# Table rows fetched by index instead of by one-hot products, and the last step of every layer norm on another engine

## The chip, the cores and the metric

The kernel runs on one core of one Trainium2 chip. A core has five engines that each work through a list of instructions of their own: TensorE (PE in the profile: matrix products, and transposes done as products with the identity), VectorE (DVE), ScalarE (ACT: activation functions and copies), GpSimd (POOL) and SyncE (SP, which here only starts transfers). Sixteen DMA engines move data. PE writes to a small accumulator memory (PSUM); everything else is in on-chip SBUF or in the chip's main memory (HBM). The metric is the time of one execution on the device in microseconds (us): the median of three runs.

## The reference, cut to what matters

One decoder layer over `x` of 4 batches x 1024 tokens x 256 features, in float32: grouped-query attention (16 heads, 4 key/value heads), cross attention to 64 context tokens, and a feed-forward stage that picks one of 64 "tiles" per token. A layer norm without scale stands before each stage, and one more with scale closes the feed-forward stage:

```python
x = x + attn(layernorm(x))            # 16 heads of 64, softmax over 1024 keys
x = x + cross_attn(layernorm(x), ctx) # 16 heads of 16, 64 keys
x = x + ffn(layernorm(x))

def ffn(xf):                          # per token
    cluster = argmax(calibrate(xf @ cluster_sigs.T))        # of 8
    local   = argmax(calibrate(xf @ sigs.T)[cluster])       # of 8
    tile    = cluster * 8 + local
    comp = tanh(gelu(xf @ w1c + b1c) @ w2c + b2c)           # 2 numbers
    hh   = relu(comp @ spline_w1[tile] + spline_b1[tile])   # 16 numbers
    mag  = hh @ spline_w2[tile] + spline_b2[tile]
    y    = xf + mag * directions[tile] * output_scale
    return layernorm(y) * gamma + beta
```

All parameters of one tile are laid in one row of `table`: 2x16 + 16 + 16 + 1 + 256 = 321 numbers, 64 rows.

## The kernel before

Tokens are worked on in tiles of 128. For each batch, layer norm 1 (`normed`, groups of two tiles) gives the transposed input `xT`; `queries`, `keys` and `value_rows` project it. `duo(b, d)` is the unit of attention: four heads of one token tile. PE makes the scores (L577), DVE the row maxima (L591), ACT the exponentials (L597); the weights are then transposed, in three duos of four by DVE in 32x32 blocks (L606) with sixteen SP transfers that carry the blocks to their place (L633), in the fourth by PE (L616) with ACT copies (L620); PE multiplies them with the values (L656). `project` (L709 to L716) closes a token tile. Every two token tiles `cross_attention` follows (layer norm 2), every four `feed_forward` (layer norms 3 and 4; two tiles at a time for the last four of the last batch). So there are nine calls of `feed_forward`, seven of four tiles and two of two.

The parts that the change touches:

- `layernorm` (L390 to L416) is three tasks. `stats` on DVE gives mean and variance of each tile (L401, L402). `rsqrt` on POOL adds eps (L406) and raises to the power -1/2 (L407). `apply` on DVE computes (x - mean) * rs, one instruction of 128x256 a tile (L412). It is called 16 times with two tiles for layer norm 1, 16 times with two for layer norm 2, 32 times with one for layer norm 3 and 32 times with one for layer norm 4: 96 calls, 128 tiles.
- `feed_forward` (L991 to L1155): after the routing, `hot` holds for each token a one-hot row of 64 (L1075). PE transposes it (`flip_hot`, L1089), ACT copies it out (L1092), and per token tile PE multiplies it with `tab`, the table in SBUF (L1097), which picks the row of 321 numbers; ACT copies that to `par` (L1100). DVE then evaluates the spline (L1116 to L1127), adds the result to the stage's input (L1131), and layer norm 4 follows. `finish` on POOL (L1146 to L1148) scales, shifts and adds the residual, and a POOL transfer stores the result (L1153).
- `tab` is loaded once, by SP, at L281, after the other weights and before the first residual tile and the third group of layer norm 1's input.

The order on every engine is fixed by a planner before the program runs. `Flow.add` takes for each task an engine, a planned cost in us, a key and the buffers it reads and writes; `Flow.order` (L120) then simulates the engines: it always emits the task that can start earliest, and among equals urgent tasks first, then the lowest key. `lag` is the planned time from a task's end to the moment that its result can be used by another engine. Each engine later works through its list in that order and waits where a planned time turns out too short. `places` is the number of buffers of each kind: three PSUM banks `p1` are shared by most small products, one `par`, one `hot`.

Of the kernel before, what the change touches and what calls it, by code (L numbers as in the profile page):

```python
# [10 lines left out]
F32 = mybir.dt.float32  # L11
U8 = mybir.dt.uint8
AF = mybir.ActivationFunctionType
ALU = mybir.AluOpType
# [3 lines left out]
P = 128  # L18
# [10 lines left out]
NTILES, NCL, TPC, GRID, COMP, NK = 64, 8, 8, 16, 64, 8  # L29
NS = NCL + NTILES  # L30
GW = 4 * GRID + 1
GT = GW + D
# [160 lines left out]
def decoder(  # L193
# [21 lines left out]
    nc = tc.nc  # L215
    const = ctx.enter_context(tc.tile_pool(name="const", bufs=1))
    big = ctx.enter_context(tc.tile_pool(name="big", bufs=1))
    work = ctx.enter_context(tc.tile_pool(name="work", bufs=2))
    small = ctx.enter_context(tc.tile_pool(name="small", bufs=4))
# [4 lines left out]
    mm, flip = nc.tensor.matmul, nc.tensor.transpose  # L224
# [1 line left out]
        dict(  # L226
            s=2, p1=3, o=1, x=3, xn1=2, xT=1, kT0=1, kT1=1, vn=4, qT=12, prob=2, probT=2, sums=3, nmax=4,
            heads=1, rb=1, rsum=2, res=1, ln=2, xxT=1, xqT=1, kblk=1, vblk=1, xkt=1, xvt=1, xsc=1,
            xmx=2, xpT=1, xrs=2, xo=1, xoT=1, xf=1, fxT=1, hT=1, sc=1, comp=2, cal=1, fm=4, hot=1, hotT=1,
            par=1, hh=1, mag=2,  # L230
        ),
        {"p1", "ln", "res", "rb", "rsum", "nmax"},
    )
    add = flow.add

# [4 lines left out]
    def psum1(name):  # L240

        return Buf("p1", lambda: ps_1.tile([P, 512], F32, tag="p1", name=name))
# [4 lines left out]
    def load(name, shape, src, engine, key, lag, dtype=F32, via=None):  # L247
        t = const.tile(shape, dtype, name=name)
        b = Buf()
        q = nc.sync if engine == "SP" else nc.scalar  # L250
        for k, (dst, s) in enumerate(via(t, src) if via else [(t, src)]):
            add(engine, 0.5, key, lambda dst=dst, s=s: q.dma_start(out=dst, in_=s), writes=[b], lag=lag)
        return t, b
# [24 lines left out]
    sraw, sraw_ = weight("sraw", sig_rawT, DC, NTILES, "SP", -33, 8)  # L278
    cw1, cw1_ = weight("cw1", c_w1, DC, COMP, "SP", -32, 8)
    cw2, cw2_ = load("cw2", [COMP, 2], c_w2, "SP", -31, 8)  # L280
    tab, tab_ = load("tab", [NTILES, GT], table, "SP", -30, 8)  # L281

    def row(name):
        a, b = ROW_AT[name]
# [105 lines left out]
    def layernorm(key, name, src, dst, w, reads, writes):  # L390

        st = Buf("ln", lambda: (
            small.tile([P, w, 6], F32, tag="bnst", name=f"{name}_st", bufs=2),
            small.tile([P, w, 2], F32, tag="bnmv", name=f"{name}_mv", bufs=2),
            small.tile([P, w], F32, tag="bnrs", name=f"{name}_rs", bufs=2),
        ))

        def stats():
            bn, mv, _ = st.t
            for t in range(w):  # L400
                nc.vector.bn_stats(bn[:, t, :], src(t))  # L401
                nc.vector.bn_aggr(mv[:, t, :], bn[:, t, :])  # L402

        def rsqrt():
            _, mv, rs = st.t
            nc.gpsimd.tensor_scalar(rs, mv[:, :, 1], EPS, None, ALU.add)  # L406
            nc.gpsimd.tensor_tensor(rs, rs, minus_half.to_broadcast([P, w]), ALU.pow)  # L407

        def apply():
            _, mv, rs = st.t  # L410
            for t in range(w):
                nc.vector.tensor_scalar(dst(t), src(t), mv[:, t, 0:1], rs[:, t : t + 1], ALU.subtract, ALU.mult)  # L412

        add("DVE", 0.6 * w, key, stats, reads, [st], holds=writes)
        add("POOL", 1.0, key, rsqrt, [st], [st])
        add("DVE", 0.41 * w, key, apply, [st, *reads], writes)  # L416

    def transposed(key, name, src, dst, k, reads, write):

# [131 lines left out]
    def duo(b, d):  # L551
# [3 lines left out]
        if e == 0:  # L555
            sums[b, qt] = buf("sums", small, H, name=f"sums_{b}_{qt}")
            heads[b, qt] = buf("heads", work, QC, P, name=f"heads_{b}_{qt}")
        ss = sums[b, qt]
        prob = Buf("prob", lambda: work.tile([P, 4 * S], F32, tag="prob", name=f"prob_{b}_{d}"))
        probT = Buf("probT", lambda: work.tile([P, 4 * S], F32, tag="probT", name=f"probT_{b}_{d}"))  # L560

# [84 lines left out]
        for part in range(2):  # L646
            def values(part=part):
                for kc in range(4 * part, 4 * part + 4):
                    for z, r in enumerate(halves):
                        j = 2 * jp + z  # L650
                        if by_array(d):
                            rhs = probT.t.rearrange("p (z c x) -> p z c x", z=2, c=NT)[:, z, kc]
                        else:
                            rhs = probT.t.rearrange("p (b z i c q) -> p b z i c q", b=4, z=2, i=2, q=32)[:, :, z, :, kc]
                            rhs = rhs.rearrange("p b i q -> p i b q")
                        mm(  # L656
                            av.t[r, :],
                            lhsT=vns[b, kc // 2].t[:, kc % 2, j * HD : (j + 1) * HD],
                            rhs=rhs,
                            start=(kc == 0),  # L660
                            stop=(kc == NT - 1),
                        )

            add(
                "PE", 1.9, at + 1, values,
                [probT.part((z, part)) for z in range(2)] + [vns[b, 2 * part], vns[b, 2 * part + 1]] + [av] * part,
                [av],
                holds=[heads[b, qt]],
            )

        rs = buf("rsum", small, 4, name=f"rsum_{b}_{d}")
# [319 lines left out]
    def feed_forward(b, t0, w, at):  # L991
# [50 lines left out]
        def route():  # L1042
# [18 lines left out]
        hot = Buf("hot", lambda: (  # L1061
            small.tile(wide, F32, tag="hot", name=f"hot_{name}", bufs=1),
            small.tile([P, w, TPC], F32, tag="sel", name=f"sel_{name}", bufs=2),
        ))

        def c_wide():
            return ch.t[1].unsqueeze(3).to_broadcast(wide)

        def select():
            h, sel = hot.t  # L1070
            nc.vector.tensor_tensor(h, sc.t[:, :, NCL:].rearrange("p t (c j) -> p t c j", j=TPC), c_wide(), ALU.mult)
            nc.vector.tensor_reduce(sel, h.rearrange("p t c j -> p t j c"), AX.X, ALU.add)

        def chosen():
            nc.vector.tensor_tensor(hot.t[0], lh.t[1].unsqueeze(2).to_broadcast(wide), c_wide(), ALU.mult)  # L1075

        add("DVE", 1.0, at + 6, select, [sc, ch], [hot])
        c, gates = calibrated(at + 7, f"cl_{name}", lambda: hot.t[1], w, [hot])
# [1 line left out]
        add("DVE", 0.45, at + 9, chosen, [lh, ch, hot], [hot])  # L1080


        hotT = Buf("hotT", lambda: big.tile([NTILES, n], F32, tag="hotT", name=f"hotT_{name}"))
        par = Buf("par", lambda: big.tile([P, w, GT], F32, tag="par", name=f"par_{name}"))
        pt = psum1(f"pht_{name}")

        def flip_hot():
            for k in range(w):
                flip(pt.t[:NTILES, k * P : (k + 1) * P], hot.t[0][:, k].rearrange("p c j -> p (c j)"), ident)  # L1089

        add("PE", 0.14 * w, at + 10, flip_hot, [hot], [pt], holds=[hotT])
        add("ACT", 0.6, at + 10, lambda: nc.scalar.copy(hotT.t, pt.t[:NTILES, :n]), [pt], [hotT])  # L1092
        for t in range(w):
            pg = psum1(f"pg_{name}_{t}")

            def gather(t=t, pg=pg):
                mm(pg.t[:, :GT], lhsT=hotT.t[:, t * P : (t + 1) * P], rhs=tab, start=True, stop=True)  # L1097

            def evict(t=t, pg=pg):
                nc.scalar.copy(par.t[:, t, :], pg.t[:, :GT])  # L1100

            add("PE", 0.6, at + 11, gather, [hotT, tab_], [pg], holds=[par])
            add("ACT", 0.45, at + 11, evict, [pg], [par.part(t)])


        hh = Buf("hh", lambda: (
# [169 lines left out]
```

## Time and profile before

The median of three runs is 1993.22 us (1990.15 to 1993.29). The profiled execution took 1997.92 us, 1996.2 us of it from its first to its last instruction (the span).

| | busy us | share of the span | instructions |
|---|---|---|---|
| PE, matrix products | 1864.4 | 93% | 11204 |
| DVE | 1538.9 | 77% | 2447 |
| ACT | 964.2 | 48% | 1730 |
| POOL | 267.2 | 13% | 422 |

How to read the lines that follow: a group of instructions is named by line, engine, operation and tile, `out<-in`, with partitions x elements of each, the number of instructions, then the busy time and the mean of one in ns, and then the time that the engine had stood idle just before them and what ended it. The chain of work that ended last is followed back from the last instruction, at each step to what released it. In a timeline the first two numbers are start and duration in us, and square brackets hold the idle time before. PEclk is the granted clock of PE, where 1.00 is full speed.

### The profile page before, as it was taken

How to read it: one execution, taken by the hardware profiler on the slowest of the kernel's cores; microseconds unless marked ns; L12 is line 12 of the kernel's file. 1: busy time of each engine (PE TensorE's matmuls, PEld its weight loads, DVE VectorE, ACT ScalarE, POOL GpSimd, SP SyncE). 2: the span in 40 equal slices, each digit the busy share in tenths (PEclk: the TensorE clock that was granted, in tenths of full speed). 3: DMA queues.
4: the chain of work that ended last, by engine and by line, in shares of the span. 5: the costliest groups of instructions: out<-in, count | busy, mean ns of one | idle time of the engine just before them, and what ended most of it. 6: DMA issues, size and time to landing. Idle time of an engine off the chain costs nothing.

```text
span 1996.2 us, 30371 instructions
## 1 busy us (share of the span) xinstructions
PE 1864.4 (93%) x11204; PEld 1114.0 (56%) x11204; DVE 1538.9 (77%) x2447; ACT 964.2 (48%) x1730; POOL 267.2 (13%) x422
## 2 busy tenths in 40 slices
PE   7899999999999999989999999989999999997973
PEld 4455555655566555556556555655556655564542
DVE  4767787897788878787778878887778877778853
ACT  2545455555445555545445545454545554553431
POOL 1000101030010301121000311103001030010322
PEclk9899999999999999989999999998999999998975
DMA  3555554454455455545454456535455435545510
GB/s 132 127 127 137 127 132 109 105 121 108 104 127 117 94 122 123 123 110 127 96 116 107 95 128 137 122 75 127 96 122 127 101 91 127 113 100 127 119 24 5
DMA packets 87859, 220.92 MB, mean 111 GB/s; under 512 B 26336, under 2 KB 36896, under 8 KB 87712
## 3 DMA queue, kind: packets, MB, share of 16 engines
q1 hardware_dynamic: 85440, 212.42, 47.3%
q0 software_dynamic: 1168, 4.19, 0.6%
q8 instruction: 89, 1.46, 0.3%
q10 hardware_dynamic: 1104, 2.37, 0.3%
q14 instruction: 58, 0.48, 0.1%
HBM read 13.37 MB, written 4.19 MB: 9 GB/s over the span
## 4 chain that ended last, share of the span: by engine, by line
PE 81%; DVE 12%; ACT 3%; DMA 1%; issue 1%; SPq 1%; POOL 1%; POOLq 0%; ACTq 0%; DVEq 0%
PE s L577 25%; PE av L656 22%; DVE nmax L591 6%; PE pq L530 5%; PE po L709 5%; PE ptp L616 5%; PE rb L682 2%; PE xav L870 2%; PE xs L819 2%; PE pxq L797 2%; ACT prob L597 2%; PE pv L502 2%; DVE prob L606 1%; PE pk L479 1%; PE pg L1097 1%; PE pxp L900 1%
## 5 line engine op out<-in xcount | busy, mean ns | idle before, releaser
L597 ACT ACTIVATE prob<-s,nmax 128x1024 f32<-128x1024 f32 x512 | 569.2, 1115 | 581.0 <-DVE nmax L591 571.3
L591 DVE TENSOR_REDUCE nmax<-s 128x1 f32<-128x1024 f32 x512 | 602.1, 1217 | 211.4 <-PE s L577 210.6
L577 PE MATMUL s<-kT,qT 64*128 64x512 f32 x2048 | 545.4, 621 | 9.3 <-ACT prob L597 9.0
L656 PE MATMUL av<-probT,vn 128*64 128x256 f32 x4096 | 479.6, 385 | 2.7 <-DMA probT<-prob 2.5
L606 DVE STREAM_TRANSPOSE prob<-prob 128x1024 f32<-128x1024 f32 x384 | 460.3, 1225 | 20.5 <-ACT prob L597 15.3
L656 PEld LDWEIGHTS av<-probT,vn 128*64 128x64 f32 x4096 | 284.0, 137 | 204.1 <-issue 70.5
L577 PEld LDWEIGHTS s<-kT,qT 64*128 64x128 f32 x2048 | 196.2, 187 | 216.6 <-issue 170.2
L620 ACT COPY probT<-ptp 128x512 f32<-128x512 f32 x256 | 138.9, 594 | 127.7 <-PE ptp L616 127.7
L616 PE MATMUL ptp<-ident,prob 128*128 128x128 f32 x1024 | 147.6, 281 | 20.5 <-ACT probT L620 5.0
L616 PEld LDWEIGHTS ptp<-ident,prob 128*128 128x128 f32 x1024 | 109.9, 141 | 76.4 <-issue 31.2
L530 PE MATMUL pq<-ln_T,wq 128*128 128x256 f32 x512 | 132.2, 407 | 4.2 <-DMA wq<-in_w_qT 3.7
L837 POOL TENSOR_TENSOR xsc<-xsc,xmx 128x1024 f32<-128x1024 f32 x32 | 61.0, 1908 | 497.0 <-DVE xmx L834 252.6
L709 PE MATMUL po<-wo,heads 128*128 128x256 f32 x512 | 121.1, 386 | 1.9 <-DVE xsc L822 1.8
L530 PEld LDWEIGHTS pq<-ln_T,wq 128*128 128x128 f32 x512 | 99.2, 202 | 32.8 <-issue 15.0
L709 PEld LDWEIGHTS po<-wo,heads 128*128 128x128 f32 x512 | 94.2, 190 | 34.5 <-issue 15.9
L715 POOL TENSOR_TENSOR x<-x,res 128x256 f32<-128x256 f32 x32 | 23.3, 728 | 620.9 <-DVE res L712 516.6
L597 ACT ACTIVATION_READ_ACCUMULATOR prob<-s,nmax 128x1 f32 x512 | 100.8, 197 | 0.0
L541 ACT ACTIVATE qT<-pq,bqs,qscale 128x256 f32<-128x256 f32 x128 | 65.3, 563 | 49.6 <-PE pq L530 49.2
L695 DVE TENSOR_TENSOR heads<-av,rb 128x256 f32<-128x256 f32 x128 | 53.0, 414 | 46.7 <-PE av L656 45.6
L682 PEld LDWEIGHTS rb<-ident,rsum 128*64 128x64 f32 x1024 | 54.6, 136 | 59.0 <-issue 45.4
L682 PE MATMUL rb<-ident,rsum 128*64 128x128 f32 x1024 | 83.3, 284 | 4.2 <-DVE xres L903 4.2
L819 PE MATMUL xs<-kblk,xq 128*128 128x512 f32 x128 | 67.9, 653 | 1.7 <-ACT xq L806 1.7
(162 smaller groups left out, 1526.9 us busy)
## 6 DMA issues: line engine op xcount, KB each, us to landing
probT<-prob SPq DMA_DIRECT2D x1536, 128.0 KB, 2.3
ln_n<-in_x SPq DMA_DIRECT2D x16, 256.0 KB, 3.1
x<-in_x SPq DMA_DIRECT2D x8, 512.0 KB, 4.2
out<-ln_n POOLq DMA_DIRECT2D x7, 512.0 KB, 3.5
wo<-in_w_oT SPq DMA_DIRECT2D x1, 1024.0 KB, 13.3
wq<-in_w_qT ACTq DMA_DIRECT2D x1, 1024.0 KB, 9.6
rowv<-in_rows ACTq DMA_DIRECT2D x1, 774.0 KB, 11.7
xwkv<-in_xw_kv SPq DMA_DIRECT2D x1, 512.0 KB, 13.1
```

The lines of the kernel that those rows point to most:

```text
L530: mm(pq.t[:, 2 * P * k : 2 * P * (k + 1)], lhsT=wq[:, dc, (c + k) * P : (c + k + 1) * P], rhs=xTs[b].t[:, dc, 2 * P * w : 2 * P * (w + 1)] ...
L541: nc.scalar.activation(qTs[b, w, c + k].t, pq.t[:, 2 * P * k : 2 * P * (k + 1)], AF.Identity, bias=bqs[:, c + k : c + k + 1], scale=qscale,)
L577: mm(ps[z].t[:, 512 * g : 512 * (g + 1)], lhsT=q.t[r, (qt % 2) * P : (qt % 2 + 1) * P], rhs=kT.t[r, 512 * g : 512 * (g + 1)], start=True, ...
L591: nc.vector.tensor_reduce(nmax.t, ps[z].t, AX.X, ALU.max, negate=True)
L597: nc.scalar.activation(weights(prob.t, z, i), src, AF.Exp, bias=nmax.t, accum_out=ss.t[:, k : k + 1])
L606: nc.vector.transpose(t, t)
L616: flip(pt.t[:, j * P : (j + 1) * P], weights(prob.t, z, i)[:, kc * P : (kc + 1) * P], ident)
L620: nc.scalar.copy(to[:, z, 4 * g : 4 * g + 4, i, :], pt.t.rearrange("p (c q) -> p c q", q=P))
L656: mm(av.t[r, :], lhsT=vns[b, kc // 2].t[:, kc % 2, j * HD : (j + 1) * HD], rhs=rhs, start=(kc == 0), stop=(kc == NT - 1),)
L682: mm(pr.t[r, i * P : (i + 1) * P], lhsT=rs.t[:, k : k + 1].to_broadcast([P, HD]), rhs=ident, start=True, stop=True,)
L709: mm(po.t[:, :D], lhsT=hT.t[:, c, :], rhs=wo[:, c, :], start=(c == 0), stop=(c == QC - 1))
L819: mm(ps.t, lhsT=qT.t[:, c, k * P : (k + 1) * P], rhs=kblk.t[:, c], start=True, stop=True)
```

## The change

Two parts, and what goes with them.

- The one-hot row is not made any more. `chosen` computes the number of the tile instead, 72 - 8*a - b with a and b the two "falling" values of the maxima, and writes it as an integer. The transposes, the 64x321 products and both ACT copies go; per token tile POOL starts an indirect DMA that fetches, for each of the 128 tokens, the row of `table` in HBM that the integer names, straight into `par`. The planner is told 1.2 us of POOL for one and 3.0 us until it has landed. `tab` and its load go.
- `apply` of every layer norm becomes an ACT activation, Identity(rs * x + bias) with per-partition scale and bias. The bias, -mean * rs, takes two more POOL instructions in `rsqrt`; its planned cost stays at 1.0 us. The planned 0.41 us a tile on DVE become 0.45 on ACT.

The name `hd` and the changed order of a set of names alter nothing that is emitted.

```diff
-            ... hot=1, hotT=1,
+            ... hot=1,
             par=1, hh=1, mag=2,
         ),
-        {"p1", "ln", "res", "rb", "rsum", "nmax"},
+        {"p1", "ln", "res", "rsum", "nmax", "rb"},
...
-    tab, tab_ = load("tab", [NTILES, GT], table, "SP", -30, 8)
...
         def rsqrt():
             _, mv, rs = st.t
             nc.gpsimd.tensor_scalar(rs, mv[:, :, 1], EPS, None, ALU.add)
             nc.gpsimd.tensor_tensor(rs, rs, minus_half.to_broadcast([P, w]), ALU.pow)
+            nc.gpsimd.tensor_tensor(mv[:, :, 1], mv[:, :, 0], rs, ALU.mult)
+            nc.gpsimd.tensor_scalar(mv[:, :, 1], mv[:, :, 1], -1.0, None, ALU.mult)
 
         def apply():
             _, mv, rs = st.t
             for t in range(w):
-                nc.vector.tensor_scalar(dst(t), src(t), mv[:, t, 0:1], rs[:, t : t + 1], ALU.subtract, ALU.mult)
+                nc.scalar.activation(dst(t), src(t), AF.Identity, bias=mv[:, t, 1:2], scale=rs[:, t : t + 1])
...
-        add("DVE", 0.41 * w, key, apply, [st, *reads], writes)
+        add("ACT", 0.45 * w, key, apply, [st, *reads], writes)
...
             small.tile([P, w, TPC], F32, tag="sel", name=f"sel_{name}", bufs=2),
+            small.tile([P, w], F32, tag="tno", name=f"tno_{name}", bufs=1),
+            small.tile([P, w], mybir.dt.int32, tag="tile", name=f"tile_{name}", bufs=1),
...
         def chosen():
-            nc.vector.tensor_tensor(hot.t[0], lh.t[1].unsqueeze(2).to_broadcast(wide), c_wide(), ALU.mult)
+            _, _, no, idx = hot.t
+
+            nc.vector.scalar_tensor_tensor(no, ch.t[0], float(-TPC), lh.t[0], ALU.mult, ALU.subtract)
+            nc.vector.tensor_scalar(idx, no, float(NCL * TPC + NCL), None, ALU.add)
...
-        hotT = Buf("hotT", lambda: big.tile([NTILES, n], F32, tag="hotT", name=f"hotT_{name}"))
         par = Buf("par", lambda: big.tile([P, w, GT], F32, tag="par", name=f"par_{name}"))
-        pt = psum1(f"pht_{name}")
-
-        def flip_hot():
-            for k in range(w):
-                flip(pt.t[:NTILES, k * P : (k + 1) * P], hot.t[0][:, k].rearrange("p c j -> p (c j)"), ident)
-
-        add("PE", 0.14 * w, at + 10, flip_hot, [hot], [pt], holds=[hotT])
-        add("ACT", 0.6, at + 10, lambda: nc.scalar.copy(hotT.t, pt.t[:NTILES, :n]), [pt], [hotT])
         for t in range(w):
-            pg = psum1(f"pg_{name}_{t}")
-
-            def gather(t=t, pg=pg):
-                mm(pg.t[:, :GT], lhsT=hotT.t[:, t * P : (t + 1) * P], rhs=tab, start=True, stop=True)
-
-            def evict(t=t, pg=pg):
-                nc.scalar.copy(par.t[:, t, :], pg.t[:, :GT])
-
-            add("PE", 0.6, at + 11, gather, [hotT, tab_], [pg], holds=[par])
-            add("ACT", 0.45, at + 11, evict, [pg], [par.part(t)])
+            def gather(t=t):
+                nc.gpsimd.indirect_dma_start(
+                    out=par.t[:, t, :],
+                    out_offset=None,
+                    in_=table,
+                    in_offset=bass.IndirectOffsetOnAxis(ap=hot.t[3][:, t : t + 1], axis=0),
+                )
+
+            add("POOL", 1.2, at + 11, gather, [hot], [par.part(t)], lag=3.0)
```

## The prediction

> **What bounds the kernel now.** I read the page's busy times first, then the chain that ended last, then the busy times by stretch.
>
> ```profile
> PE 1864.4 (93%) x11204; PEld 1114.0 (56%) x11204; DVE 1538.9 (77%) x2447; ACT 964.2 (48%) x1730; POOL 267.2 (13%) x422
> ```
>
> ```profile
> PE 81%; DVE 12%; ACT 3%; DMA 1%; issue 1%; SPq 1%; POOL 1%; POOLq 0%; ACTq 0%; DVEq 0%
> ```
>
> ```profile
> 60.00:1900.00 1840.00, 1769.14 (x10797) 1052.70 (x10796) 1464.50 (x2218) 921.74 (x1654) 239.84 (x355) 0.98 0.51 115
> 1900.00:1996.20 96.20, 51.33 (x242) 33.04 (x240) 41.41 (x146) 22.93 (x42) 21.66 (x33) 0.67 0.02 8
> ```
>
> The columns of the last view are PE, weight loads, DVE, ACT and POOL busy, then granted clock and DMA share. From 60 to 1900 us PE is busy for 1769 of 1840 us, so PE time taken away there is worth nearly its full length, unless PE then waits for something else. The last 96 us are different: no engine is full, the clock is 0.67, and each step waits for the one before it. There, latency counts.
>
> The groups that the change removes or moves, the nearest rows for what it adds, and PE's longest wait:
>
> ```profile
> L1097 PE MATMUL pg<-tab,hotT 64*128 64x321 f32 x64 | 30.3, 604 | 4.3 <-ACT hotT L1092 2.2 <-DVE rb L691 1.2 <-ACT par L1100 0.8
> L1089 PE MATMUL pht<-ident,hot 128*64 128x128 f32 x32 | 6.3, 322 | 30.1 <-DVE hot L1075 30.1
> L1100 ACT COPY par<-pg 128x321 f32<-128x321 f32 x32 | 13.2, 432 | 22.1 <-PE pg L1097 21.8
> L412 DVE TENSOR_SCALAR ln_n<-x,ln_mv,ln_rs 128x256 f32<-128x256 f32 x64 | 24.2, 400 | 10.7 <-POOL ln_rs L407 10.7
> L541 ACT ACTIVATE qT<-pq,bqs,qscale 128x256 f32<-128x256 f32 x128 | 65.3, 563 | 49.6 <-PE pq L530 49.2
> L406 POOL TENSOR_SCALAR ln_rs<-ln_mv 128x1 f32<-128x1 f32 x64 | 14.0, 218 | 116.7 <-DVE ln_mv L402 109.9 <-DVE rsum L676 6.8
> L1153 POOL DMA_DIRECT2D out<-ln_n x9 | 7.6, 848 | 2.4 <-POOL ln_n L1148 2.4
> ```
>
> ```profile
> PE pht L1089 <- DVE hot L1075: 15.5, 3, 9.6
> ```
>
> That wait, 60 to 1900 us, is three waits for the one-hot row in three of the seven four-tile calls of feed-forward. PE's timeline shows one:
>
> ```profile
> 869.83 0.66 PE L1089 MATMUL pht<-ident,hot 128*64 128x128 f32 x4 [2.93 <-DVE hot L1075]
> 871.16 4.64 PE L1097 MATMUL pg<-tab,hotT 64*128 64x321 f32 x8 [0.67 <-ACT hotT L1092]
> 875.74 1.11 PE L426 MATMUL ln_pt<-ident,ln_n 128*128 128x128 f32 x4
> ```
>
> The eight products take 4.64 us here, 3.16 in the first call (390 to 420 us): between 872 and 880 us the clock is 0.50.
>
> **What the Trainium skill says.** (1) "ScalarE: Activation LUTs", section "What ACT_TABLE_LOAD costs": 186 ns + 0.833 ns an element, about 93 ns more for each per-partition operand, and 93 ns of overlap back to back. For 256 elements with scale and bias that is an estimate of 585 ns; the trace has 563 (L541, the same form, though from PSUM). Its section on table sets says that identity comes with every set; the trace agrees, L541 runs among exponentials and only 19 table loads exist. (2) "DMA: Bandwidth & Descriptors", "Anatomy of one DMA — SWDGE (gpsimd) path": 2.0 us + bytes/436 GB/s. The trace's two POOL stores, 512 KB in 3.5 us and 256 KB in 2.6, are near it (3.2 and 2.6). (3) "SBUF — State Buffer", "SBUF: two separate sides": DVE and POOL share a port pair as an exclusive lock, which can also hold up the descriptors of a POOL transfer. The trace agrees as to the lock: L985, 0.18 us elsewhere, takes 0.72 at 1919.44 beside a POOL add. (4) "TensorE: Matmul & The Clock Gate", Part 1: after an idle window of some 3.4 us PE runs at half speed until it has been busy for as long; the 0.50 above agrees.
>
> **The change part by part**, against the profiled execution (span 1996.2, 1997.9 with what lies around it).
>
> *Part 1, PE's share of the table lookup.* Seven calls of four tiles lie in the full stretch. In calls 1, 2, 4 and 6 PE is not waiting for the one-hot row: `pht` takes 0.63 each and the eight `pg` 3.2, 3.1, 3.3 and 3.6 (PE's busy time of these tiles by stretch; call 2 has six in the stretch at 2.33 and two before it), together 15.7, with about 0.8 of idle time for the two evictions of `par` in three of the calls (0.28 each). Worth -16.5.
>
> Calls 3, 5 and 7 are DVE-bound: DVE is busy for 3.9 of every 4 us up to the one-hot row, and PE's next work, the transpose `ln_pt` of layer norm 2, needs statistics that DVE makes after it. So the PE wait doesn't go; what counts is when `ln_pt` can start. In call 3 the statistics end at 870.76. POOL then takes 0.31 + 0.71 for two tiles, plus two new small instructions at 0.22 with a gap of 0.08 (L406's row): 1.6 us, 872.5. ACT takes 1.05 for two tiles: 873.6, against 875.74 before: -2.1. Call 5 is its copy, -2.1. In call 7 (1805 to 1824 us) the statistics end at 1817.6, which by the same steps gives `ln_pt` at 1820.3 instead of 1823.6, -3.3, and the `pg` behind it, 2.7, go as well. Sum -10.2. Against it: a gather may stand before that POOL work, since both become ready within 1.2 us and the plan gives a gather 1.2. I charge 1.0 a call, +3. Worth -7.
>
> *The gather itself* isn't in this trace. Issue on POOL: no cheaper than the direct store's 0.85, and at most three times that, 2.5 (128 rows named by data). Landing: 164 KB by the skill's price, 2.4; by this trace's POOL stores at most 3.5. I take 1.0 and 2.4. Queued behind four of them (4 us) on POOL are the power of other layer norms, the subtraction L837, the residual adds and `finish`; ACT and DVE wait for those. POOL is busy 13%, which is the cover. At the upper ends `par` lands 10 + 3.5 us after the index, where the plan gives 7.8: DVE would stand 5.7 us before the spline.
>
> *Part 2, layer norms.* DVE loses 24.2 + 19.1 + 12.2 = 55.5 us (the three shapes of L412), and L1075's 0.40 becomes two small ones of about 0.2. ACT gains 128 x 0.51 to 0.56 = 65 to 72, and loses 13.2 + 4.9 of copies (L1092 is 0.58 x 7 + 0.37 x 2): 48% becomes 51%. POOL gains 96 x 0.6 = 58 and 32 gathers: 13% becomes 18%. What shows on the path: DVE is 12% of the chain, so I take 12% of 55, -6. Each normalised tile comes later, 0.6 on POOL and 0.15 on ACT, and the plan doesn't know of the 0.6, so ACT will stand waiting for POOL with exponentials behind it. PE has attention to do meanwhile; from 60 to 1900 us it waited for `ln_n` for only 2.8 us. I take 5% of 96 x 0.8, +4. Together -2; the ends are -15 and +45 (see the last rival).
>
> *Start.* SP's `tab` issue, 0.53 us at 17.57, stands before the input that DVE waits for until 23.23: -0.6.
>
> *Tail.* What the last call does between index and spline:
>
> ```profile
> 1978.54 0.62 PE pht L1089 x2
> ...
> 1979.18 0.37 ACT hotT L1092
> ...
> 1979.60 2.52 PE pg L1097 x4
> ...
> 1982.14 0.43 ACT par L1100
> ```
>
> From 1978.40, when the one-hot row is there, to 1982.60: 4.2 us. New: two issues and one landing, 2 x 1.0 + 2.4 = 4.4 (3.7 to 8.5): +0.2. Layer norm 4's two tiles go through POOL one after the other, so four extra instructions: +1.2. Layer norm 3 of the last tile: +0.75. Layer norm 2 at 1921: its transpose no longer waits for `pg` (to 1923.88), but comes at 1924.4 by POOL and ACT, later if the two gathers go first: +1.1. Sum +3.3.
>
> Sum: -16.5 - 7 - 2 - 0.6 + 3.3 = -22.8, 1.1% of the span. The median, 1993.2, stands 4.7 below the profiled time; the same step from it gives 1970.
>
> **Rivals.** *The stalls go whole* (15%): the plan is made anew, and attention comes to stand where PE now idles. In calls 3, 5 and 7 that frees the waits 15.5 + 1.3, `pht` 2.7, `pg` 12.0 and the half-speed excess of what follows (pxq 1.4 and 1.8, xs 1.8, av 2.4), 39 instead of 7: 1938 if all, 1948 at two thirds. For: these are the three longest waits of PE. Against: DVE is full there. *DVE waits for the gather* (17%): a gather of twice the plan's figures makes `par` 4 x 1.2 + 3 = 7.8 us late; 7 x 7.8 = 55 us on DVE, of which two fifths reach PE, and the gain is gone: 1992. For: the DMA engines are 0.9 busy from 1346 to 1362 us. Against: the tail's store lands in 2.6. *ACT blocks behind POOL* (slower, 10%): the 0.6 us that the plan doesn't know, in 96 layer norms, sits in front of exponentials; if all passes to PE it costs 58, not the 4 above, and the time is 2024; at half, 1998. It decides from 27 us on, 0.28 of the 0.6. For: PE waited 33 + 7 us for L597 in the full stretch, so exponentials are near the path. Against: ACT is idle half the time. The rest, 58%, is the forecast with its own range of 1957 to 1983.
>
> **How the numbers follow.** A difference of 0.2%, 4 us, is about what can be told from none. Range: the forecast's own (58%), the larger gain down to 1946 (10 of its 15), the gather case up to 1994 (13 of its 17): 81%. Faster: 57 + 15 + 7 of the gather case = 79%; same: 1 + 5 + 1 = 7%; slower: 5 of the gather case and 9 = 14%.
>
> **What would show it.** Right: PE's busy time 30 to 37 us less with neither `pht` nor `pg`; no wait for L1075 on PE; DVE near 1485, ACT near 1015, POOL near 360; the span from 60 us to the last score product shorter by 25; the tail 3 us longer. Wrong: gathers over 2 us on POOL; DVE waiting for the transfer into `par` for more than 2 us a call; ACT waiting for POOL's `ln_rs` for tens of us with PE waiting for L597 longer than 40; or new waits of PE as long as the three of before, at places that the new plan chose.

## The result and the profile after

The changed kernel takes 2009.14 us (median of six runs, 2005.38 to 2010.05) beside 1994.64 for the kernel before (six runs, 1990.15 to 1998.52). The ratio is 1.006, 95% interval 1.0044 to 1.0077: slower by 0.6%, some 12 us by the ratio (the two medians differ by 14.5). The forecast was 1970. The profiled execution took 2008.93 us with a span of 2007.0.

Busy times of the changed kernel, from its page:

```profile
PE 1847.6 (92%) x11108; PEld 1106.8 (55%) x11108; DVE 1487.0 (74%) x2328; ACT 1014.0 (51%) x1817; POOL 342.9 (17%) x646
```

The work went where it was meant to go: DVE has 52 us less, ACT 50 more, POOL 76 more. But PE has only 17 us less, and the span is 11 longer, so PE's idle time grew by 28 us. The stretches of the changed kernel, with columns as before (PE, weight loads, DVE, ACT, POOL, granted clock, DMA share):

```profile
60.00:1900.00 1840.00, 1749.76 (x10669) 1043.11 (x10668) 1417.72 (x2115) 962.33 (x1726) 306.07 (x553) 0.98 0.51 117
1900.00:2007.00 107.00, 53.77 (x274) 35.44 (x272) 40.46 (x142) 27.94 (x49) 29.24 (x51) 0.68 0.10 25
```

Counted from the last score product, at 1897.1 us before and at 1903.9 now, the loss is 6.8 us in the long stretch and 4.0 in the tail.

The groups that are new (of the `ln_n` step the 64 tiles that are read from `x`, which are those of layer norms 2 and 3), and from the list of transfers what the gather takes from issue to landing (its last number, median us):

```profile
L1093 POOL DMA_INDIRECT par<-in_table,tile x32 | 32.9, 1028 | 79.7 <-DVE tile L1082 73.7 <-issue 5.9
L413 ACT ACTIVATE ln_n<-x,ln_mv,ln_rs 128x256 f32<-128x256 f32 x64 | 36.7, 597 | 76.0 <-POOL ln_mv L408 76.0
```

```profile
par<-in_table,tile POOLq DMA_INDIRECT x32, 5.0
```

A gather costs POOL 1.03 us, which is the 1.0 of the forecast. Its landing isn't: 5.0 us instead of 2.4. One activation takes 0.60 us, and ACT stood idle for 76 us in front of these 64, each time for the last of POOL's four small instructions. For all three groups of the step, and the whole trace, that wait is

```profile
ACT ln_n L413 <- POOL ln_mv L408: 124.4, 63, 14.2
```

PE's waits between 60 and 1900 us (total, number, longest), first in the changed kernel, then the same waits before:

```profile
PE s L579 <- ACT prob L599: 16.6, 16, 2.8
PE ptp L618 <- ACT probT L622: 15.7, 18, 2.2
PE ln_pt L427 <- ACT ln_n L413: 10.3, 5, 3.3
PE rb L684 <- DVE xres L905: 9.2, 11, 0.8
PE av L658 <- DMA probT<-prob: 6.3, 4, 3.1
```

```profile
PE s L577 <- ACT prob L597: 7.2, 7, 2.0
PE ptp L616 <- ACT probT L620: 4.2, 15, 0.5
PE ln_pt L426 <- DVE ln_n L412: 2.8, 3, 0.9
PE av L656 <- DMA probT<-prob: 2.5, 2, 1.9
```

The wait for the one-hot row, 15.5 us before, is gone. In its place stand many waits of up to three microseconds for ACT and for the carried blocks of `probT`.

### The profile page after: what moved, and what is told of

It reads as the page before. It is cut to its first block, busy times and chain, and to the rows that moved or that the text cites. A ratio compares the mean times of both kernels' runs of the same rounds, so it can differ in the third digit from the quotient of the medians.

```text
span 2007.0 us, 30493 instructions
## 1 busy us (share of the span) xinstructions
PE 1847.6 (92%) x11108; PEld 1106.8 (55%) x11108; DVE 1487.0 (74%) x2328; ACT 1014.0 (51%) x1817; POOL 342.9 (17%) x646
## 5 line engine op out<-in xcount | busy, mean ns | idle before, releaser
L579 PE MATMUL s<-kT,qT 64*128 64x512 f32 x2048 | 557.2, 628 | 16.9 <-ACT prob L599 16.6
L579 PEld LDWEIGHTS s<-kT,qT 64*128 64x128 f32 x2048 | 200.4, 189 | 235.2 <-issue 176.7
L531 PE MATMUL pq<-ln_T,wq 128*128 128x256 f32 x512 | 125.7, 391 | 3.3 <-ACT ln_T L430 3.3
L711 PEld LDWEIGHTS po<-wo,heads 128*128 128x128 f32 x512 | 93.6, 190 | 35.9 <-issue 21.4
L531 PEld LDWEIGHTS pq<-ln_T,wq 128*128 128x128 f32 x512 | 94.7, 192 | 29.5 <-issue 13.4
L684 PEld LDWEIGHTS rb<-ident,rsum 128*64 128x64 f32 x1024 | 56.0, 137 | 61.5 <-issue 36.6
L427 PE MATMUL ln_pt<-ident,ln_n 128*128 128x128 f32 x192 | 38.9, 319 | 39.3 <-ACT ln_n L413 27.6
```

The lines of the kernel that those rows point to most:

```text
L531: mm(pq.t[:, 2 * P * k : 2 * P * (k + 1)], lhsT=wq[:, dc, (c + k) * P : (c + k + 1) * P], rhs=xTs[b].t[:, dc, 2 * P * w : 2 * P * (w + 1)] ...
L579: mm(ps[z].t[:, 512 * g : 512 * (g + 1)], lhsT=q.t[r, (qt % 2) * P : (qt % 2 + 1) * P], rhs=kT.t[r, 512 * g : 512 * (g + 1)], start=True, ...
L684: mm(pr.t[r, i * P : (i + 1) * P], lhsT=rs.t[:, k : k + 1].to_broadcast([P, HD]), rhs=ident, start=True, stop=True,)
L711: mm(po.t[:, :D], lhsT=hT.t[:, c, :], rhs=wo[:, c, :], start=(c == 0), stop=(c == QC - 1))
```

## The experiments

All ratios are to the kernel before, with 95% intervals. Three theories stood at the start. In theory L the steps moved to ACT and POOL come later, and PE waits for them (the first four texts below call it theory N). In theory O the planner's new order is the cause. In theory G the gather itself costs what it saves.

### Each part alone, each in an order of its own

The gather alone is the changed kernel with this undone and the two bias instructions taken out:

```diff
-                nc.scalar.activation(dst(t), src(t), AF.Identity, bias=mv[:, t, 1:2], scale=rs[:, t : t + 1])
+                nc.vector.tensor_scalar(dst(t), src(t), mv[:, t, 0:1], rs[:, t : t + 1], ALU.subtract, ALU.mult)
...
-        add("ACT", 0.45 * w, key, apply, [st, *reads], writes)
+        add("DVE", 0.41 * w, key, apply, [st, *reads], writes)
```

> The gather of table rows as in the changed kernel, the layer norms as before (applied on DVE, two POOL instructions). Theory N (the layer norms' longer way over POOL and ACT costs the time, the gather by itself gains): 14 to 30 us faster than before, 1965 to 1981. Theory G (the gather, which lands 5 us after its issue, takes the gain back): no faster than before, 1993 to 2010. Theory O (any new list of orders loses at the places where batches meet, whichever part made it): within 8 us of before either way, and PE idle longer between the last tile of a batch and the second call of feed-forward.

1995.49 us, ratio 1.0008 (0.9996 to 1.0021): no difference.

The layer norms alone are the kernel before with the opposite edit and the two bias instructions:

> The layer norms as in the changed kernel (bias on POOL, applied on ACT), the table lookup by one-hot products as before. Theory N: slower than before by 20 to 45 us, 2015 to 2040, since no PE work goes. Theory G: within 5 us of before, or up to 10 faster because DVE loses 55 us of work. Theory O: 5 to 15 us slower.

2021.01 us, ratio 1.0133 (1.0097 to 1.017). So the layer norms make the loss and the gather makes no gain. The prediction had both otherwise, and each needs its reason.

### Shorter latency, and truer costs for the planner

The first takes the two bias instructions out and gives the mean itself as the bias. The subtraction of the mean is thus left out; the lists are otherwise those of the changed kernel.

```diff
-            nc.gpsimd.tensor_tensor(mv[:, :, 1], mv[:, :, 0], rs, ALU.mult)
-            nc.gpsimd.tensor_scalar(mv[:, :, 1], mv[:, :, 1], -1.0, None, ALU.mult)
...
-                nc.scalar.activation(dst(t), src(t), AF.Identity, bias=mv[:, t, 1:2], scale=rs[:, t : t + 1])
+                nc.scalar.activation(dst(t), src(t), AF.Identity, bias=mv[:, t, 0:1], scale=rs[:, t : t + 1])
```

> The changed kernel without the two POOL instructions that make the bias; the activation takes the mean itself as its bias, so the subtraction of mean times scale is left out of the computation. The planned costs are the same, so every engine has the same list otherwise. Theory N with the latency as its cause: 0.6 us less in each of 96 layer norms gives back 8 us or more, under 2001. If the order sets the time and not the latency: 2 to 4 us faster than the changed kernel (the tail's share alone), 2005 to 2007.

2003.75 us, ratio 1.0038 (1.0022 to 1.0053): about 5 us of the 12, and the intervals of the two overlap a little. It lies between the two statements.

The second leaves every instruction as it is and tells the planner 1.6 us for `rsqrt`, 0.57 a tile for the activation and 5.0 for the landing, as measured:

```diff
-        add("POOL", 1.0, key, rsqrt, [st], [st])
-        add("ACT", 0.45 * w, key, apply, [st, *reads], writes)
+        add("POOL", 1.6, key, rsqrt, [st], [st])
+        add("ACT", 0.57 * w, key, apply, [st, *reads], writes)
...
-            add("POOL", 1.2, at + 11, gather, [hot], [par.part(t)], lag=3.0)
+            add("POOL", 1.2, at + 11, gather, [hot], [par.part(t)], lag=5.0)
```

> The changed kernel, with the planner told what its trace measured: 1.6 us for the POOL part of a layer norm, 0.57 a tile for its ACT part, 5.0 us until a gather has landed. Nothing else changes, but the plan is made anew. Theory N through a plan that is blind to the new latency: back to before or better, under 1995. Theory O: anywhere within 10 us of the changed kernel. Theory G: DVE's wait for the gathers goes and some 5 us with it.

2050.95 us, ratio 1.0295 (1.0254 to 1.0336). Truer costs made it 42 us slower than the changed kernel, which no theory had named. Order alone can move the time by more than the whole change did, so instructions and order have to be measured apart.

### The same lists, other instructions

The planner's costs, engines and dependencies are those of before, and only what a task issues is changed. The step of a layer norm is planned on DVE and issued on ACT. The gather is issued where the table's product stood, and the product's tasks issue nothing. TensorE's list in these kernels is the list of before, entry by entry, without `pht` and `pg` where the gather takes their place.

```diff
         def apply():
...
-                nc.vector.tensor_scalar(dst(t), src(t), mv[:, t, 0:1], rs[:, t : t + 1], ALU.subtract, ALU.mult)
+                nc.scalar.activation(dst(t), src(t), AF.Identity, bias=mv[:, t, 1:2], scale=rs[:, t : t + 1])
...
         add("DVE", 0.41 * w, key, apply, [st, *reads], writes)
```

```diff
-        add("PE", 0.14 * w, at + 10, flip_hot, [hot], [pt], holds=[hotT])
+        add("PE", 0.14 * w, at + 10, None, [hot], [pt], holds=[hotT])
...
             add("PE", 0.6, at + 11, gather, [hotT, tab_], [pg], holds=[par])
-            add("ACT", 0.45, at + 11, evict, [pg], [par.part(t)])
+            add("ACT", 0.45, at + 11, None, [pg], [par.part(t)])
```

(`gather` is now the indirect DMA.) Both parts, the layer norms alone, and the gather alone:

> Both parts of the change, with every instruction where the list of before has it: the normalising step issued on ScalarE where the VectorE instruction stood, the gathers where the table's products stood, the planner's costs those of before. TensorE's list is that of before without the table's products. If the new order made the loss (theory O): 1970 to 1990, faster than before, since the 34 us of table products are gone and nothing else of TensorE's list moved. If the ScalarE step's own latency behind GpSimd makes it (theory L): 2000 to 2012, like the changed kernel.

> The layer norms as in the changed kernel, the table's products kept, TensorE's list exactly that of before. Theory O: within 8 us of before (1990 to 2002). Theory L: as slow as the layer norms alone in their own order, 2012 to 2024.

> The gather alone, issued where the table's products stood, layer norms as before, the planner's costs those of before. Theory O: 1968 to 1985, below the gather in its own new order (1995), and as fast as both parts in the old order. Theory L, in which the gather's gain is lost because ln_T and probT simply come no earlier: 1990 to 1997, as in the new order.

The converse issues the instructions of before in the order that is planned for layer norms on ACT:

> The converse: the instructions of before (normalising step on VectorE, no bias instructions, table's products kept) in the order that the planner makes for layer norms on ScalarE. TensorE's list is that of the run with the layer norms alone, 2021 us. Theory O: 2012 to 2024, slow with nothing of the change in it but the order. Theory L: 1990 to 2000.

| | order of before | order planned for it |
|---|---|---|
| layer norms on ACT | 2019.06, 1.0115 (1.0074 to 1.0156) | 2021.01, 1.0133 |
| layer norms on DVE | before | 2027.51, 1.0155 (1.0114 to 1.0196), in the order planned for ACT |
| gather | 1997.04, 0.9995 (0.9983 to 1.0007) | 1995.49, 1.0008 |
| both | 2023.86, 1.0133 (1.0083 to 1.0182) | 2009.14, 1.006 |

Theory O falls as the cause of the loss: in the order of before the whole change is slower still, 1.0133 against 1.006, and these intervals don't touch. Replanning gave half of it back. Moving the layer norms costs 22 us with PE's list untouched, which speaks for theory L, though its statement for both parts, 2000 to 2012, is too low. Yet the order planned for ACT is a bad one by itself: with nothing of the change in it, it costs 30 us.

With the layer norms on ACT in the order of before, PE waits from 60 to 1880 us show:

```profile
PE s L579 <- ACT prob L599: 11.2, 13, 2.5
PE ln_pt L428 <- ACT ln_n L414: 6.7, 12, 1.1
```

and ACT itself:

```profile
ACT ln_n L414 <- POOL ln_mv L409: 53.9, 36, 2.9
```

ACT works through its list in the planned order. It stands for 54 us before normalising steps that POOL isn't ready for, and the exponentials behind them come later: PE's wait for them goes from 7.2 to 11.2 us. PE's wait for `ln_n` goes from 2.8 to 6.7 in the same view. These two come to 8 of the 17 us by which the span of this execution is longer; 3 more are in the tail.

### Which layer norms

In the order of before, the step moved only for layer norms 3 and 4 (64 tiles), then only for 1 and 2 (64 tiles, two to a call, so 32 calls; the expectations below count these as 32 of 96, which is calls, not tiles), the bias instructions with them:

```diff
+                if name[:3] in ("ln3", "ln4"):
+                    nc.scalar.activation(dst(t), src(t), AF.Identity, bias=mv[:, t, 1:2], scale=rs[:, t : t + 1])
+                else:
                     nc.vector.tensor_scalar(dst(t), src(t), mv[:, t, 0:1], rs[:, t : t + 1], ALU.subtract, ALU.mult)
```

> In before's own order, with the table's products: the normalising step goes to ScalarE (and GpSimd gets the two bias instructions) only in the feed-forward's norms ln3 and ln4, 64 of the 96 tiles. If ScalarE is held up because GpSimd's root stands behind the long finishing products there (theory F): 2008 to 2016, most of the 22 us that all norms cost in this order. If every moved step costs alike (theory A, about 0.23 us for each tile): 2008 to 2014 too, but then the next run takes the rest, 2001 to 2006. If it is the attention's norms (theory N): 1992 to 2000.

> The same for the other norms alone, ln1 and ln2, 32 of the 96 tiles, whose result TensorE transposes at once. Theory F: 1993 to 2000. Theory A: 2001 to 2006. Theory N: 2010 to 2018.

2005.76 us, ratio 1.0039 (1.0024 to 1.0055), and 2012.8, ratio 1.008 (1.0052 to 1.0109). They add up to the 1.0115 of both. For as many tiles norms 1 and 2 cost about twice as much: by the ratios 16 us (10 to 22) against 8 (5 to 11). Theory F, which expected most of it from the feed-forward, doesn't describe this; N, which put all of it on the attention, is nearer. Theory A isn't settled. It expected two thirds from the feed-forward by the wrong count; with 64 tiles on either side it says 11 us for each, which is at the edge of both intervals.

Nor does ACT's wait behind POOL tell the price. From 60 to 1880 us it is, with norms 3 and 4 on ACT and then with norms 1 and 2:

```profile
ACT ln_n L416 <- POOL ln_mv L410: 44.8, 29, 2.9
```

```profile
ACT ln_n L416 <- POOL ln_mv L410: 10.6, 8, 2.2
```

The shorter wait goes with the higher price. PE transposes the tiles of norms 1, 2 and 3, not those of norm 4. One place, the same in both traces, first before, then with norms 1 and 2 on ACT:

```profile
743.03 0.78 PE L426 MATMUL ln_pt<-ident,ln_n 128*128 128x128 f32 x4 [0.93 <-DVE ln_n L412]
```

```profile
751.21 0.33 PE L432 MATMUL ln_pt<-ident,ln_n 128*128 128x128 f32 x1 [1.11 <-ACT ln_n L416]
```

PE's idle time in the clock record (3.41 us of granted clock) around this place is 1.28 us instead of 0.93, and yet the next record, from 753.1 to 756.5 us, is at half speed in the second trace and not in the first. Taken over the trace (for each clock record, the share of speed not granted times PE's busy time in it), half speed costs PE 45.7 us before and 58.6 here: 13 of the 22 us by which the span of this profiled execution is longer (the medians differ by 16). PE's idle time is 5 us longer. With all norms on ACT half speed costs 46.9, hardly more than before, and PE's idle time is 11 us longer. So half speed is what this one execution lost, and not shown to be the rule.

### Order alone

The kernel before, with nothing changed but one number given to the planner:

```diff
-        add("DVE", 0.41 * w, key, apply, [st, *reads], writes)
+        add("DVE", 0.45 * w, key, apply, [st, *reads], writes)
```

> The kernel before, instruction for instruction, but the planner is told 0.45 us instead of 0.41 for the normalising step, which stays on VectorE; so only the order of the instructions differs. If the order alone, changed by nothing that matters, moves the time as much as the whole change did (theory O): 10 us or more either way, below 1985 or above 2005. If small changes of order even out: 1989 to 2001.

2003.64 us, ratio 1.0047 (1.0028 to 1.0065): 7 us by the medians, 6 to 13 by the interval. It is clearly more than nothing; whether it reaches the 10 that theory O named isn't settled.

### Why the gather gains nothing

In the order of before, PE is busy for 1831.9 us, 32 less than before, and the time doesn't move. PE's waits (60 to 1880 us) and DVE's waits (whole span) of that kernel:

```profile
PE av L656 <- DMA probT<-prob: 24.9, 10, 10.3
PE ln_pt L426 <- DVE ln_n L412: 21.9, 8, 5.7
```

```profile
DVE hh L1118 <- DMA par<-in_table,tile: 25.6, 7, 6.1
```

First guess (theory D): DVE paces these calls. The calibration's knots were left out in both kernels, 30 us of DVE's work by the trace, 25 of it before 1900 us:

```diff
-        for cost, do in (..., (1.0, lambda: picked(0)), (1.0, lambda: picked(1)), (0.4, value)):
+        for cost, do in (..., (1.0, None), (1.0, None), (0.4, value)):
```

> The kernel before, in its own order, without the look-up of the calibration's knots (two products and two sums over the knots, 3.7 us of VectorE for each calibration pair of a four-tile call; the calibrated value is then wrong, since this part is left out). Theory D, that VectorE paces the feed-forward calls: the 26 us of VectorE work come back in good part, 1972 to 1988, the tail's share being 5 us. If TensorE paces them (theory T): 1987 to 1994, only the waits for the one-hot rows and the tail gain.

> The same omission in the kernel with the gather in the old order (1997). Theory D: once VectorE is ahead, taking the table's products from TensorE pays, so this is 12 to 30 us below the last run: 1950 to 1972. Theory T: the gather still gains nothing because what waits is the transposed probabilities and the gather's landing: within 6 us of the last run, 1982 to 1996.

1994.48 us, ratio 0.9988 (0.9978 to 0.9999), and 1991.37, ratio 0.9958 (0.9944 to 0.9973). Theory D falls: DVE's work is worth 3 us in one kernel and 6 in the other, near the statements of theory T, that TensorE paces them. In the second, PE still waits 5.71 us for `ln_n` in the third call, as with all the work.

Second guess (theory C): the gather itself. The same kernel without any look-up, the parameters read from the normalised tile, nothing put in place of the gathers:

```diff
-            def gather(t=t):
-                nc.gpsimd.indirect_dma_start(...)
-            add("PE", 0.6, at + 11, gather, [hotT, tab_], [pg], holds=[par])
+            add("PE", 0.6, at + 11, None, [hotT, tab_], [pg], holds=[par])
...
-            p = par.t
+            p = xf.t
```

> The gather in the old order (1997), but with no gather at all: the parameters are read from the normalised tile at once, so the look-up itself is left out and nothing stands in its place; every list is otherwise the same. Theory C, that the gather's own transfers hold up the transposed probabilities (they land in 4.2 us beside it, 2.3 without) and VectorE waits for its landing: 1970 to 1985. Theory S, that the table's products stood in a stretch whose length TensorE doesn't set, since the next normalised tiles and scores come no earlier: 1990 to 1997, hardly better than with the gather, and TensorE's wait for ln_n stays above 15 us.

1975.35 us, ratio 0.9901 (0.9868 to 0.9934). Theory C holds: taking the products away is worth 20 us by the ratio (23 by the medians), and the gather costs 19 of them (22 by the medians). Theory S named one thing rightly, PE's wait for `ln_n`, which stays; the gain comes all the same. The waits without a gather, same view:

```profile
PE ln_pt L426 <- DVE ln_n L412: 21.9, 8, 5.7
PE av L656 <- DMA probT<-prob: 12.2, 3, 10.4
```

Half of the wait for `probT` is gone, and 10.4 us of what is left are one wait in the seventh call. The transfers into `probT` between 862 and 892 us, around the third call, from issue to landing, in the kernel with the gather (12 of its 32 have a landing in the trace):

```profile
DMA to landing us min/median/max: 2.3/4.2/5.6
```

and in the kernel without a look-up, all 32:

```profile
DMA to landing us min/median/max: 2.3/2.3/4.0
```

Before it was 2.3 too. The carried blocks of attention weights take nearly twice as long beside four gathers, and in the kernel with the gather PE stands there, in the third call:

```profile
882.59 3.67 PE L656 MATMUL av<-probT,vn 128*64 128x256 f32 x32 [2.41 <-DMA probT<-prob]
```

The Trainium skill ("DMA: Bandwidth & Descriptors", section "SWDGE vs HWDGE vs iDMA") says that transfers issued by POOL and by SP go through the same sixteen DMA engines, each of which takes turns between the queues. The traces agree as far as they go: from 868 to 885 us the sixteen engines are busy for 0.96 of the time with the gather and for 0.86 without a look-up. The taking of turns isn't seen.

The tail, from the last score product, is 99.1 us before, 103.7 with the gather and 93.6 without a look-up. Set side by side score product by score product, the kernel with the gather falls behind the one without in the stretch just behind calls 3 to 6 above all, by 6.5, 5.2, 5.3 and 2.1 us of the 19 that it is late at the last one; in all four places PE waits for `probT` first, 2.2 to 3.4 us. The tail adds 10. So these two executions, whose spans differ by 29, tell where the price is paid. How it divides between slowed `probT` transfers, DVE's wait for `par` and POOL's 33 us of issuing wasn't tried apart.

### Versions meant to be faster

The gather alone, with the table's products kept in the last two calls:

```diff
+        if w == TX:
+            ...  # pht, pg and their copies as before
+        else:
             for t in range(w):
```

> The gather alone, layer norms as before, but the last two calls, of two tiles each, keep the table's products. The gather alone ended its last score product 9.6 us before the kernel before and lost 5.6 us in the tail; without the gather in the tail that part should be as before: 1982 to 1990, faster than both kernels. If the tail's loss isn't the gather's, or the new order undoes the gain: 1993 to 2003.

1993.91 us, ratio 0.9987 (0.9974 to 1.0001): not told from no change. The tail took 104.7 us in both kernels, so that loss wasn't the gather's in this order.

With the gather, the last step of layer norm 4 on GpSimd instead of DVE, in the order of before and in its own:

```diff
-                nc.vector.tensor_scalar(dst(t), src(t), mv[:, t, 0:1], rs[:, t : t + 1], ALU.subtract, ALU.mult)
+                e = nc.gpsimd if name[:3] == "ln4" else nc.vector
+                e.tensor_scalar(dst(t), src(t), mv[:, t, 0:1], rs[:, t : t + 1], ALU.subtract, ALU.mult)
```

> The gather in the old order, and the normalising step of the feed-forward's last norm (ln4) as the old instruction on GpSimd, just behind the root that it waits for; ScalarE gets nothing, VectorE loses 13 us. Theory D: 1980 to 1993, the calls get shorter. If GpSimd's own products come late for it, or the shared port takes it back: 1996 to 2010.

> The same with the planner told of the gather and of GpSimd's step (0.6 us), so in an order of its own. From the gather in its own order, 1995: theory D 1978 to 1992. As an order changed for no reason moved the time by 7 us, anything from 1985 to 2005 says little of the step itself.

2007.32 us, ratio 1.005 (1.003 to 1.0071), and 1994.04, ratio 0.9981 (0.9966 to 0.9996). A step moved in an unchanged list costs here too, 10 us on top of the gather, with no ACT in it. The instruction takes 1237 ns on GpSimd against 400 on DVE, and the planner had been told 0.6. Planned, it is 0.2% faster than the kernel before, the only complete version of all that was measured faster; at that size it is hardly more than a draw of the order.

Layer norm 2 marked as urgent in that last kernel:

```diff
-        add("DVE", 0.6 * w, key, stats, reads, [st], holds=writes)
+        add("DVE", 0.6 * w, key, stats, reads, [st], holds=writes, urgent=name[:3] == "ln2")
```

(and likewise `rsqrt` and `apply`)

> The gather in its own order with ln4's last step on GpSimd (1994), and the cross attention's norm ln2 marked as urgent for the planner, so that its normalised tile, for which TensorE waits in each feed-forward call, comes sooner. If that wait is what eats the gather's gain: 1975 to 1988 and TensorE's wait for ln_n below 8 us. If the wait only moves on, or the scores' maxima come later for it: 1990 to 2005.

2027.61 us, ratio 1.0178 (1.0133 to 1.0224): far outside both statements. PE's wait for `ln_n` stays, at 18.2 us, so this tells of the order again, and nothing of what the wait is worth.

## Why the prediction was wrong

- **Sum.** −22.8 forecast, about +12 measured (by the ratio). The sign was wrong, and 2009 lies outside 1946 to 1994.
- **Table products, calls 1, 2, 4 and 6: −16.5.** The cover was judged rightly and the size too high. With nothing in place of the products, in the same lists, 10 us are gained across these calls (1.2, 1.3, 2.2 and 5.2), read from the starts of the score products before and after each.
- **Calls 3, 5 and 7: −10.2, less 3 for a gather in the way.** The kernel without a look-up gains 9.2 over the three calls, which is near by luck: 2.8, 5.5 and 0.9 where 2.1, 2.1 and 6.0 were forecast. In calls 3 and 5 the mechanism holds: PE now waits for `ln_n`, and the time from its work before the wait to `ln_pt` shrinks (call 3: −3.1 us; −2.1 was worked out with the longer way through ACT). In call 7 it fails. PE's next work there is not `ln_pt` but the product with the values, and the 9.65 us for the one-hot row had covered an equal wait for `probT`:

```profile
1797.93 6.61 PE L656 MATMUL av<-probT,vn 128*64 128x256 f32 x32 [10.36 <-DMA probT<-prob]
```

- **The gather: no price beyond 3 us, landing 2.4.** This step failed. The landing was taken from the price for a direct transfer that the prediction cites, with POOL's direct stores (3.5 and 2.6 us) beside it, and was to be hidden. It measured 5.0, and what the sum had no term for was that `probT` transfers land later beside a gather, and PE waits for them: 24.9 us with it, 12.2 without. The price in the order of before is 19 to 22 us, all that part 1 gains; in the new order it wasn't measured with nothing in the gather's place. The rival "DVE waits for the gather", 1992, named the size and half of the mechanism. In the changed kernel the planner has moved DVE's wait out of the way (10.9 us, 9.9 of it in the tail), but its median landing of `probT` around the third call is still 3.5.
- **Layer norms: −2.** This step failed too, inside its stated ends of −15 and +45: the delay of the normalised tiles was put at 4 us. DVE's relief, 12% of 55 us (which is 6.7, not 6), isn't what failed; 30 us less on DVE, in the run with the shortened calibration, brought 3, a like share. ACT's waits behind POOL were in the forecast, but as "tens of us" with PE's wait for the exponentials over 40 only among the signs of its being wrong. Both came: 124 us, and 17 + 47 us (products + weight loads) against the 7 + 33 that the prediction names. In the order of before the move costs 22 us; in the changed kernel, against the gather alone, about 10. As a net share of the delay (96 x 0.8) that is near 30% and 13%, not 5%. The rival "ACT blocks behind POOL", given 10%, has the gather's gain in hand (its half case is 1995 by its own sum, not 1998); without that gain some 10 of its 58 us give this result. That ACT's waits as such are the price isn't shown, since the two halves of the norms contradict it.
- **The order.** The forecast took a better plan as a rival and new waits at places of the plan's choosing as a sign, but had no term for a worse one. Replanning the whole change is worth −0.7% here, and other plans of the same instructions moved the time by up to +2.3% (the truer costs, against the changed kernel).
- **Start −0.6, tail +3.3.** The start is right, −0.7 at the first score product. The tail, +4.0 from the last one on, is right by luck in part: in the order of before the norms alone lengthen it by 3.2, as forecast (3.05), but the gather alone by 4.6, where 0.2 was forecast, and both together by 9.4; the new order took the rest back.
- **Signs in the profile.** DVE 1485, ACT 1015: measured 1487 and 1014. POOL 360: 343. PE less by 30 to 37: 17. The rows of `pht` and `pg` were 36.6 us, 10.2 of it lost to half speed; but half speed at other places grew from 35.5 to 49.6 us, so that 14 came back there. Some 6 us aren't accounted for. The middle part is 7 longer, not 25 shorter.

What stays open: by what way the moved layer norms cost 22 us, and whether norms 1 and 2 really cost twice what norms 3 and 4 cost; half speed after slightly longer waits is seen in one trace and not tried by itself. Also open is how the gather's price divides.

## What to carry to other kernels

Before crediting a saving, run the kernel with the work left out and nothing in its place, then with the replacement: the difference is the replacement's price, and here it was the whole saving, paid at least in part by waits for transfers that nobody counted as neighbours. Where a planner fixes the order, change the instructions in the old order and the order with the old instructions; one edit that does both can't be read. A step handed from one in-order engine to another is not free because the new engine is half idle: look at what is queued behind it there.

## What the runs showed of the hardware

Idle time of PE well below a clock record already goes with lost speed. The granted clock comes in records of 3.41 us. Over all twenty traces, between 60 and 1890 us, after a record at full speed the next was at half speed in 1 of 9029 cases where PE had been idle for under 0.5 us in the record (in one wait or several), in 11 of 869 at 0.5 to 1.0, 33 of 168 at 1.0 to 1.5, 55 of 104 at 1.5 to 2.0, and in all 134 at 2.0 or more. Many of these cases are the same place in several runs. The section of the Trainium skill that the prediction cites ("TensorE: Matmul & The Clock Gate", Part 1) speaks of an idle window of some 3.4 us; by these traces 2 us of idleness within a record were always enough, and 1 to 2 us in a third of the cases. An estimate from these figures: a record at half speed loses up to 1.7 us of work, so a wait of 2 us that falls into one record costs nearly twice its length, and one that grows across 1 us can cost more than its growth.

An indirect DMA of 128 rows of 1284 bytes takes 1.03 us of GpSimd and lands 5.0 us after its issue (median of the changed kernel). Around four of them, transfers of blocks between SBUF tiles land in 4.2 us instead of 2.3 (medians; 12 landings in the trace with the gather, 32 in the one without).
